# Value matmuls of two key steps in one run, one pair of adds by accumulating DMA, and a later normalisation, in a transformer block on one core

## The chip, the core and the metric

The kernel runs on one core of a Trainium2 chip. The core has a matrix engine (TensorE, PE in the profile, its weight loads as PEld), a vector engine (VectorE, DVE), an activation engine (ScalarE, ACT), a general engine (GpSimd, POOL) and a queue engine that only issues transfers here (SyncE, SP). Each takes its instructions in the order of its own queue and waits on semaphores for the others. The metric is the device time in microseconds; the median of three runs before is 1076.01 us (1075.66 to 1076.06).

## The reference

All data are float32. There are 2 sequences of 1024 tokens of width 512, 16 heads of 32, and a mixture of 8 experts with a shared one.

```python
q, k, v = (split(x @ W.T + b + 0.5 * (x @ Bm.T) @ Am.T) for W, b, Bm, Am in qkv)
attn = softmax(q @ k.T * HEAD_DIM ** -0.5)
x = layernorm(x + lora_linear(merge(attn @ v), Wo, bo, Bo, Ao))
# then: top-1 of 8 experts with capacity 256, gated, plus a shared expert
x = layernorm(x + moe(x))
```

## The kernel before

The program has three stages: the projections to q, k and v (about the first 160 us), attention (to about 628 us), and the experts. The change touches attention alone.

**Units and steps.** Attention runs over 16 units `u`: a group of four heads, `g = u // 2`, and one half of the queries (512 of them). A unit has 8 steps `kc`, one for each block of 128 keys; the loop at the end of the attention stage counts `t = 8 u + kc` up to 127. The order of the work is written out by hand: within this loop all five engines keep the order in which the program issues (`tc.manual_schedule(engines=MAN2)`), so every engine's queue is what the Python code says.

**What a step does.** `st_step` makes four score tiles, one per head: a matmul writes `st` (128 keys x 512 queries) into one of three PSUM banks of the pool `one`, and ScalarE writes its exponential into half of an exponential tile `pt` (128 x 2 x 512, two heads). Such tiles come from a pool of `PTB` buffers; `pts[t, pr]` is the tile of head pair `pr` at step `t`. Between the four heads other work is queued, in the lists `between[0]` to `between[3]`:

- `s1_step` works 12 steps ahead (`LEAD`). It makes score tiles `s` of a later unit the other way round (queries on the partitions) into three PSUM banks of the pool `s1p`, and VectorE takes each row's maximum (`mt`). The maxima of a unit end in `mx`, are turned by a transpose (`mp`) and go by two small DMAs into two extra rows of the query tile `qs`, so that the later matmul `st` subtracts them. There are four such tiles per step, up to step 115.
- `av_step(t - 1)` multiplies the exponentials of the step before with the values. A head's output is only 32 wide, so four heads fill the four column groups of TensorE and share one bank `av`; eight matmul instructions of the trace are one such run. There are two banks `av`.
- `add_step` sums the exponentials of steps 1 to 6 into the tiles of step 0 (`accs`), for the denominators. For most units ten adds go to GpSimd and two to VectorE (`ON_DVE`): (step 1, pair 0), queued early, at its own step, and (step 2, pair 1). The last two units have a division of their own (`DVE_END`).
- `finish(u - 1)`, at step `FIN` of the next unit, makes the column sums with a matrix of ones: sixteen matmul instructions over the tiles of step 7 and of the sums, directly behind a value run. ScalarE copies the result to `rc`, SP sends four rows to DRAM and back as `r16`.
- `invert(u - 1)`, after step `REC`, takes the reciprocal on VectorE; SP writes it out and broadcasts it to 32 partitions per head with four DMAs, as `rb`.
- `normalize(u - 1)` at step 7 multiplies the bank `av` by it on VectorE (`mult`, part 0), ScalarE makes the rounded half `at_h` (part 1), VectorE the rest `at_l` (`lo`, part 2).
- `add_res` adds a bias to the residual rows on GpSimd, mostly once per unit at its step 1; the rows were loaded three steps earlier. `oproj` is the output projection: of the first sequence from step 65 to step 81, of the second from step 126 on.

SP also loads the keys of a later head group, the queries of a later unit and the values at the beginning of units. Line numbers of the profile: 182 the tile `s`, 190 its maximum, 569 `st`, 578 the exponential, 588 the add, 599 the value matmul, 622 the sums, 636 to 653 the copy and the reciprocal with its transfers, 661 to 665 the normalisation, 674 the bias of the residual.

Of the kernel before, what the change touches and what calls it, by code (L numbers as in the profile page):

```python
# [9 lines left out]
F32 = mybir.dt.float32  # L10
# [3 lines left out]
ALU = mybir.AluOpType  # L14
# [4 lines left out]
P = 128  # L19
B, L, D = 2, 1024, 512  # L20
NU = 16
# [13 lines left out]
NS = NU * 8  # L35
WARM, WCOL = 4, 256
OPER = 4
PTB = 13
OHB = 3
LOADS = {  # L40
# [10 lines left out]
MAN4 = MAN2 - MAN3  # L51
DIRECT = (7,)
NO_DIR = (NU - 2,)
FIN = 3
REC = 4
XTB = 5
ON_DVE = ((1, 0), (2, 1))
EARLY = (1, 0)
OPROJ_AT = (65, 67, 69, 71, 73, 75, 77, 79)
RES_AT = tuple(8 * i + 6 for i in range(8)) + (70, 78, 86, 94, 98, 102, 106, 110)  # L60
RES_ADD = 3
# [7 lines left out]
FINE, NRME = 2, 4  # L69
DVE_END = {  # L70
    NU - 2: ((1, 0), (2, 1), (4, 1), (5, 1), (6, 0), (6, 1), (7, 0), (7, 1)),
    NU - 1: ((1, 0), (2, 0), (3, 0), (4, 0), (5, 0), (6, 0), (6, 1)),
}
# [19 lines left out]
def kernel(  # L93
# [3 lines left out]
    pe, act, dve, pool, sp = nc.tensor, nc.scalar, nc.vector, nc.gpsimd, nc.sync  # L97

    def f(ap):
        return ap.bitcast(F32)  # L100
# [41 lines left out]
    def load_k(g):  # L142
        kt = Ks[g % 2]
        for blk, hl in ((0, 0), (1, 1), (2, 0)):
            sp.dma_start(
                out=f(kt[32 * blk : 32 * blk + 32]),
                in_=qk_d[1, g // NG, g % NG, hl].rearrange("(h p) t -> p h t", p=32),
            )
# [13 lines left out]
    def load_q(u):  # L162
        g, qb = u // 2, u % 2
        for blk, hl in ((0, 0), (1, 0), (2, 1)):
            sp.dma_start(
                out=f(Qs[u % 3][32 * blk : 32 * blk + 32]),
                in_=qk_d[0, g // NG, g % NG, hl].rearrange("(h p) t -> p h t", p=32)[
                    :, :, qb * 512 : qb * 512 + 512
                ],
            )  # L170

    mts, pts, avs, accs, vts = {}, {}, {}, {}, {}
# [377 lines left out]
    with ph2, tc.manual_schedule(engines={mybir.EngineType.PE}):  # L550
        ptp = att_left.enter_context(
            tc.tile_pool(name="ptp", bufs=PTB, side="left", reuse_waits="tile")
        )
        ap = ph2.enter_context(
            tc.tile_pool(name="ap", bufs=1, side="right", reuse_waits="tile")
        )
# [25 lines left out]
        def add_step(t, pr):  # L582
            u, kc = t // 8, t % 8
            if kc == 0:
                accs[u, pr] = pts[t, pr]
            elif kc not in direct(u):
                eng = dve if (kc, pr) in DVE_END.get(u, ON_DVE) else pool
                eng.tensor_tensor(accs[u, pr], accs[u, pr], pts[t, pr], ALU.add)  # L588

        def early(t, pr):  # L590
            return t // 8 not in DVE_END and (t % 8, pr) == EARLY

        def av_step(t):
            u, kc = t // 8, t % 8
            g = u // 2
            if kc == 0:
                avs[u] = avp.tile([P, 512], F32, name=f"av{u}", tag="av")
            for h in range(4):
                pe.matmul(  # L599
                    avs[u][32 * h : 32 * h + 32, :],  # L600
                    vts[g][:, kc, 32 * h : 32 * h + 32],
                    pts[t, h // 2][:, h % 2, :],
                    start=kc == 0,
                    stop=kc == 7,
                    skip_group_check=True,
                )
            for pr in range(2):
                if not early(t, pr):
                    add_step(t, pr)

        def direct(u):
            return () if u in NO_DIR else DIRECT
# [3 lines left out]
        def finish(u):  # L616
            sm = one.tile([P, 512], F32, name=f"sm{u}", tag="one")
            parts = [lambda h, k_=k_: pts[u * 8 + k_, h // 2][:, h % 2, :] for k_ in direct(u)]
            parts.append(lambda h: accs[u, h // 2][:, h % 2, :])
            for i, pf in enumerate(parts):  # L620
                for h in range(4):
                    pe.matmul(
                        sm[32 * h : 32 * h + 32, :],
                        ones32,
                        pf(h),
                        start=i == 0,
                        stop=i == len(parts) - 1,
                        skip_group_check=True,
                    )
            if u >= RDIR:  # L630
                rc = ap.tile([P, 512], F32, name=f"rc{u}", tag="rc", bufs=1)
                dve.reciprocal(rc, sm)
                fin[u] = rc
                return
            rc = ap.tile([P, 512], F32, name=f"rc{u}", tag="rc", bufs=1)
            act.copy(rc, sm)
            sd = dram.tile([4, 512], F32, name=f"sd{u}")
            sp.dma_start(out=sd, in_=rc[0:P:32, :])
            r16 = ap.tile([P, 16], F32, name=f"r16_{u}", tag="r16", bufs=1)
            sp.dma_start(out=r16, in_=sd.rearrange("h (j c) -> (h j) c", c=16))  # L640
            fin[u] = r16

        def invert(u):
            r16 = fin[u]
            rd = dram.tile([4, 512], F32, name=f"rd{u}")
            dve.reciprocal(r16, r16)
            sp.dma_start(out=rd.rearrange("h (j c) -> (h j) c", c=16), in_=r16)
            rc = ap.tile([P, 512], F32, name=f"rb{u}", tag="rb", bufs=1)
            for h in range(4):
                sp.dma_start(  # L650
                    out=rc[32 * h : 32 * h + 32, :],
                    in_=rd[h : h + 1, :].partition_broadcast(32),
                )
            fin[u] = rc

        def normalize(u, parts=(0, 1, 2)):
            g, qb = u // 2, u % 2
            cs = slice(qb * 512, qb * 512 + 512)
            hi, lo = at_h[:, g % NG, cs], at_l[:, g % NG, cs]
            if 0 in parts:  # L660
                dve.tensor_tensor(avs[u], avs[u], fin[u], ALU.mult)
            if 1 in parts:
                act.copy(hi, avs[u])
            if 2 in parts:
                dve.tensor_tensor(lo, avs[u], f(hi), ALU.subtract)
# [38 lines left out]
        def run(gen):  # L704
            for _ in gen:
                pass
# [4 lines left out]
        for t in range(NS):  # L711
            u, k = t // 8, t % 8
            if k == 0:
                if u % 2 == 0 and 2 <= u and u // 2 + 1 < B * NG:
                    load_k(u // 2 + 1)
                if u >= 1 and u + 2 < NU:
                    load_q(u + 2)
                if u % 2 and NG <= u // 2 + 1 < B * NG:
                    load_v(u // 2 + 1)
            if t in RES_AT:  # L720
                load_res(RES_AT.index(t))
            between = [[], [], [], []]
            if early(t, 0):
                between[2].append(lambda: add_step(t, 0))
            if t + LEAD < NS:
                for q in range(4):
                    between[q].append(lambda q=q: s1_step(t + LEAD, q))
            elif t + LEAD == NS:
                between[0].append(lambda: finish_max(NU - 1))
            if t:  # L730
                between[1].append(lambda: av_step(t - 1))
                if u and k == (FINE if u == NU - 1 else FIN):
                    between[1].append(lambda: finish(u - 1))
            if u:
                if k == (NRME if u == NU - 1 else 7):
                    between[0].append(lambda: normalize(u - 1, (0,)))
                    between[1].append(lambda: normalize(u - 1, (1,)))
                    between[2].append(lambda: normalize(u - 1, (2,)))
            if t - RES_ADD in RES_AT:
                between[3].append(lambda: add_res(RES_AT.index(t - RES_ADD)))  # L740
            st_step(t, between)
            if k == REC and 1 <= u < NU - 1:
                invert(u - 1)
            if t in OPROJ_AT:
                op0 = oproj(0, OPROJ_AT.index(t), OPER)
            if OPROJ_AT[0] <= t:
                next(op0, None)
            if t + 1 in OPROJ_AT[1:]:
                run(op0)
            for _, fn in [x for x in later if x[0] == 0]:  # L750
                fn()
            later[:] = [(n - 1, fn) for n, fn in later if n]
            if t - NS >= OPROJ1:
                next(op10, None)
        av_step(NS - 1)
        finish(NU - 1)
        normalize(NU - 1, (0,))
        run(op10)
# [301 lines left out]
    for st in range(NB):  # L1060
# [18 lines left out]
        if st == NB - 3:  # L1079
            reads_xd(  # L1080
                sp.dma_start(
                    out=meta, in_=xd_d[:, D : D + 2].rearrange("(j p) c -> p j c", p=P)
# [7 lines left out]
    with tc.manual_schedule(engines=MAN4):  # L1090
        last = None
        for e in range(E):
            nxt = e + 1
            hss = []
            for c in range(6):
# [32 lines left out]
                if e:  # L1128
                    for hf in range(2):
                        j = 2 * (e - 1) + hf  # L1130
# [7 lines left out]
        for hf in range(2):  # L1138
            j = 2 * (E - 1) + hf
# [65 lines left out]
```

## Time and profile before

| what | value |
|---|---|
| median of three runs | 1076.01 us |
| the profiled execution's own time | 1076.59 us |
| its span, first to last instruction | 1074.9 us |
| mean granted TensorE clock | 0.993 |
| a unit of attention (units 1 to 7, 11, 12) | 27.8 us |
| units 8 and 9, with output projections | 37.6 and 40.0 us |
| maximum of one tile `s` on VectorE | 512 x, mean 0.680 us |
| add on GpSimd | 151 x, mean 2.413 us |
| add on VectorE | 43 x, mean 2.131 us |

One execution is profiled; durations and waits come from it. A busy TensorE in the profile is not one at its peak, since matmuls are pipelined and their ends modelled; distances between starts tell more. In a row the form is: engine, line, operation, out<-in by the program's names (buffer numbers left out), shapes and count. In a timeline the first two columns are the start and the length in us, and a bracket at the end names the idle time before and who ended it. In the table by window the columns are the window, its length, then the busy time of PE, PEld, DVE, ACT and POOL with the number of instructions, the granted clock, the busy share of the DMA engines and their GB/s.

### The profile page before, as it was taken

Reading aid. Unit: us, or ns where it says so; the run is one execution under the profiler, and the core shown is the slowest. Engines: PE = TensorE matmul, PEld = TensorE weight load, DVE = VectorE, ACT = ScalarE, POOL = GpSimd, SP = SyncE. Lnnn points to the kernel's source line nnn. Section 1 sums busy time; section 2 is a strip of 40 time slices with the busy share of each in tenths; the row PEclk is TensorE's granted clock in tenths of the full one; section 3 lists DMA queues with packets and bytes.
Section 4 is the critical chain, followed back from the end, with each engine's and each line's share of the span. In section 5 each row is a group of like instructions: output and inputs, shape, how many; then the busy total and the mean of one; then the engine's idle time right before and its main releaser. Section 6 shows DMA issues by size and latency. Waiting matters only on the chain. (4 is left out here: it accounts for less than half of the span.)

```text
span 1074.9 us, 16446 instructions
## 1 busy us (share of the span) xinstructions
PE 1038.9 (97%) x5992; PEld 742.9 (69%) x5992; DVE 748.3 (70%) x1217; ACT 530.1 (49%) x1026; POOL 573.1 (53%) x379
## 2 busy tenths in 40 slices
PE   8999999999999999999999999999999999999996
PEld 6888774444444455544444369889999998888885
DVE  6732788999999987799998784233522556777762
ACT  5422215666666655556666756222222455555552
POOL 5000007888888877868899575000050045666674
PEclk8999999999999999999999999999999999999999
DMA  8866860141414242042520123000082556777731
GB/s 279 288 219 202 252 195 25 52 110 48 103 47 106 71 109 70 22 90 70 119 81 22 51 60 109 20 21 20 31 240 95 161 184 207 234 234 235 237 107 59
DMA packets 77585, 131.24 MB, mean 122 GB/s; under 512 B 14344, under 2 KB 23048, under 8 KB 77504
## 3 DMA queue, kind: packets, MB, share of 16 engines
q1 hardware_dynamic: 73664, 117.59, 37.6%
q0 software_dynamic: 3840, 12.60, 3.3%
q8 instruction: 47, 0.77, 0.3%
q14 instruction: 34, 0.28, 0.1%
HBM read 96.10 MB, written 33.80 MB: 121 GB/s over the span
## 5 line engine op out<-in xcount | busy, mean ns | idle before, releaser
L588 POOL TENSOR_TENSOR pt<-pt,pt 128x1024 f32<-128x1024 f32 x151 | 360.5, 2413 | 207.7 <-ACT pt L578 190.6
L190 DVE TENSOR_REDUCE mt<-s 128x1 f32<-128x512 f32 x512 | 323.4, 680 | 39.7 <-PE s L182 39.6
L578 ACT ACTIVATE pt<-st 128x512 f32<-128x512 f32 x512 | 270.8, 602 | 141.4 <-PE st L569 137.6
L569 PE MATMUL st<-qs,ks 98*128 98x512 f32 x512 | 215.6, 432 | 1.9 <-ACT pt L578 1.2
L182 PE MATMUL s<-ks,qs 96*128 96x512 f32 x512 | 203.0, 404 | 12.7 <-DVE mt L190 11.5
L569 PEld LDWEIGHTS st<-qs,ks 98*128 98x128 f32 x512 | 96.0, 189 | 136.4 <-issue 87.2
L817 POOL TENSOR_TENSOR w2s<-w2r,w2s 128x512 fp32r<-128x512 f32 x42 | 65.7, 1582 | 127.0 <-ACT w2s L816 103.1
L829 PE MATMUL h<-xthe,w13s 128*128 128x256 f32 x704 | 131.4, 284 | 1.5 <-DVE hs L850 1.5
L182 PEld LDWEIGHTS s<-ks,qs 96*128 96x128 f32 x512 | 97.2, 190 | 41.3 <-DVE mt L190 26.8
L829 PEld LDWEIGHTS h<-xthe,w13s 128*128 128x128 f32 x704 | 111.0, 191 | 3.0 <-DVE hs L850 2.7
L829 PE MATMUL h<-xtle,w13s 128*128 128x256 f32 x352 | 100.2, 285 | 0.0
L588 DVE TENSOR_TENSOR pt<-pt,pt 128x1024 f32<-128x1024 f32 x43 | 91.4, 2131 | 3.3 <-ACT pt L578 2.9
L599 PE MATMUL av<-pt,vt 128*32 128x512 f32 x512 | 75.0, 605 | 0.0
L599 PE MATMUL av<-pt,x1b 128*32 128x512 f32 x512 | 68.8, 609 | 0.0
L829 PEld LDWEIGHTS h<-xtle,w13s 128*128 128x128 f32 x352 | 67.3, 191 | 0.7
L977 POOL DMA_INDIRECT xd_d<-x1a,slot_i x8 | 8.0, 996 | 111.8 <-DVE slot_i L974 109.7
L873 PE MATMUL y<-w2s,hs 128*128 128x512 f32 x260 | 62.7, 394 | 2.9 <-POOL w2s L817 2.9
L873 PEld LDWEIGHTS y<-w2s,hs 128*128 128x128 f32 x260 | 47.4, 188 | 15.7 <-POOL w2s L817 6.7
L297 PE MATMUL o<-xh,wh 128*128 128x512 f32 x128 | 51.1, 399 | 3.0 <-ACT wh L271 3.0
L312 ACT ACTIVATE oh<-o,bqk_sb 128x512 fp32r<-128x512 f32 x32 | 22.0, 690 | 59.0 <-PE o L297 56.5
L297 PE MATMUL o<-xl,wh 128*128 128x512 f32 x128 | 50.9, 398 | 0.0
L297 PE MATMUL o<-xh,wl 128*128 128x512 f32 x128 | 50.9, 397 | 0.0
(819 smaller groups left out, 1758.5 us busy)
## 6 DMA issues: line engine op xcount, KB each, us to landing
qs<-qkd SPq DMA_DIRECT2D x48, 256.0 KB, 5.6
ks<-qkd SPq DMA_DIRECT2D x24, 512.0 KB, 6.8
x1a<-in_w_dram SPq DMA_DIRECT2D x24, 512.0 KB, 6.8
w2r<-in_w_dram SPq DMA_DIRECT2D x42, 256.0 KB, 3.2
qkd<-oh SPq DMA_DIRECT2D x32, 256.0 KB, 2.7
qkd<-ol SPq DMA_DIRECT2D x32, 256.0 KB, 2.6
x1b<-in_w_dram SPq DMA_DIRECT2D x16, 512.0 KB, 5.7
x1b<-in_wT_dram SPq DMA_DIRECT2D x16, 256.0 KB, 5.3
```

The source lines that it names most:

```text
L182: pe.matmul(s1, Qs[u % 3][0:96, h, qt * P : qt * P + P], Ks[g % 2][0:96, h, kh * 512 : kh * 512 + 512], start=True, stop=True,)
L190: dve.tensor_reduce(mts[u][:, c, kh : kh + 1], s1, AX.X, ALU.max)
L297: pe.matmul(o, lhs, rhs, start=k + i == 0, stop=k + i == KC + 1)
L312: act.activation(oh, o, AF.Identity, bias=bias)
L569: pe.matmul(sb, Ks[g % 2][:, h, kc * P : kc * P + P], Qs[u % 3][:, h, :], start=True, stop=True,)
L578: act.activation(pts[t, h // 2][:, h % 2, :], sb, AF.Exp, scale=SCALE)
L588: eng.tensor_tensor(accs[u, pr], accs[u, pr], pts[t, pr], ALU.add)
L599: pe.matmul(avs[u][32 * h : 32 * h + 32, :], vts[g][:, kc, 32 * h : 32 * h + 32], pts[t, h // 2][:, h % 2, :], start=kc == 0, stop=kc == 7 ...
L817: pool.tensor_tensor(hl[:, 1, :], raw, f(hl[:, 0, :]), ALU.subtract)
L829: pe.matmul(hp[:, j * 256 : j * 256 + 256], lhs, rhs[:, k, :], start=n == 0, stop=n == 11,)
L873: pe.matmul(o, lhs, rhs, start=n == 0, stop=n == 16)
L977: sc_ = pool.indirect_dma_start(out=xd_d, out_offset=bass.IndirectOffsetOnAxis(ap=slot_i[:, i : i + 1], axis=0), in_=x1[i // 8][:, i % 8, ...
```

## The change

`av_step` of two key steps is now issued together, at every even step: at step t those of t - 2 and t - 1, and after the loop those of the last two steps. The adds leave `av_step` and get a function `adds`, called at every step with a table `ADDS` by key step. In units 0 to 13 the tiles of step 4 are added to those of step 5 by two DMAs from GpSimd's queue that accumulate into their destination; step 6 is added before step 5, and the tiles of step 5, which hold both, one step later. One add in twelve stays on VectorE, (step 1, pair 0), without its early place. The last two units keep their division.

The sums move from step 3 to step 4 of the next unit (in the last unit they stay at step 2), the reciprocal from behind step 4 to behind step 5, the normalisation from step 7 of the next unit to step 0 of the one after it; in the last unit it stays at step 4 for unit 14, and unit 13's comes at its step 0. The broadcast reciprocal takes the buffer of `rc` instead of one of its own, and the exponential tiles are 14 instead of 13.

```diff
-PTB = 13
+PTB = 14
...
-FIN = 3
-REC = 4
+FIN = 4
+REC = 5
+NRM = 0
 XTB = 5
-ON_DVE = ((1, 0), (2, 1))
-EARLY = (1, 0)
+ON_DVE = ((1, 0),)
+ADDS = {
+    0: ((0, 0, 0), (0, 0, 1)), 1: ((0, 1, 0), (0, 1, 1)), 2: ((0, 2, 0), (0, 2, 1)),
+    3: ((0, 3, 0), (0, 3, 1)), 5: ((0, 4, 0), (0, 4, 1)), 6: ((0, 6, 0), (0, 6, 1)),
+    7: ((0, 5, 0), (0, 5, 1)),
+}
...
-            for pr in range(2):
-                if not early(t, pr):
+
+
+        def adds(t):
+            u, kc = t // 8, t % 8
+            if u in DVE_END:
+                for pr in range(2):
                     add_step(t, pr)
+                return
+            for v, j, pr in ADDS.get(kc, ()):
+                i = (u - v) * 8 + j
+                if i < 0 or u - v in DVE_END:
+                    continue
+                if j == 4:
+                    pool.dma_start(out=pts[i + 1, pr], in_=pts[i, pr], accum_op=ALU.add)
+                else:
+                    add_step(i, pr)
...
-            rc = ap.tile([P, 512], F32, name=f"rb{u}", tag="rb", bufs=1)
+            rc = ap.tile([P, 512], F32, name=f"rb{u}", tag="rc", bufs=1)
...
-            if early(t, 0):
-                between[2].append(lambda: add_step(t, 0))
...
             if t:
-                between[1].append(lambda: av_step(t - 1))
+                if t % 2 == 0:
+                    between[1].append(lambda: (av_step(t - 2), av_step(t - 1)))
+                between[1].append(lambda: adds(t - 1))
                 if u and k == (FINE if u == NU - 1 else FIN):
                     between[1].append(lambda: finish(u - 1))
             if u:
-                if k == (NRME if u == NU - 1 else 7):
-                    between[0].append(lambda: normalize(u - 1, (0,)))
-                    between[1].append(lambda: normalize(u - 1, (1,)))
-                    between[2].append(lambda: normalize(u - 1, (2,)))
+                for v in [u - 2] * (k == NRM and u > 1) + [u - 1] * (u == NU - 1 and k == NRME):
+                    between[0].append(lambda v=v: normalize(v, (0,)))
+                    between[1].append(lambda v=v: normalize(v, (1,)))
+                    between[2].append(lambda v=v: normalize(v, (2,)))
...
+        av_step(NS - 2)
         av_step(NS - 1)
+        adds(NS - 1)
         finish(NU - 1)
```

More of the change, by code (lines that the diff above doesn't have):

```diff
@@ L588, in add_step @@
                 eng.tensor_tensor(accs[u, pr], accs[u, pr], pts[t, pr], ALU.add)
-        def early(t, pr):
-            return t // 8 not in DVE_END and (t % 8, pr) == EARLY
         def av_step(t):
```

## The prediction

> **What bounds the kernel now.** I read the page first, its busy line and slices:
>
> ```profile
> PE 1038.9 (97%) x5992; PEld 742.9 (69%) x5992; DVE 748.3 (70%) x1217; ACT 530.1 (49%) x1026; POOL 573.1 (53%) x379
> ...
> PE   8999999999999999999999999999999999999996
> PEld 6888774444444455544444369889999998888885
> DVE  6732788999999987799998784233522556777762
> ...
> POOL 5000007888888877868899575000050045666674
> ```
>
> In slices 6 to 22 (about 160 to 600 us, the attention steps) PE, DVE and POOL are all near full; the change lives there. So I asked for the engines' busy time by unit (window, length, then PE, PEld, DVE, ACT, POOL busy):
>
> ```profile
> 355.00:382.80 27.80, 27.16 (x146) 13.08 (x145) 25.77 (x40) 17.79 (x36) 24.78 (x12) 1.00 0.26 68
> 382.80:420.40 37.60, 36.46 (x187) 20.53 (x185) 31.56 (x53) 19.46 (x38) 30.96 (x20) 1.00 0.36 80
> 420.40:460.40 40.00, 38.70 (x194) 22.09 (x194) 32.70 (x57) 21.45 (x40) 28.41 (x20) 1.00 0.19 49
> ```
>
> Units 1 to 7 and 10 to 13 are like the first line, 27.8 us; units 8 and 9 also carry output projections. Nobody has more than 3 us free. The PE timeline shows where a step goes:
>
> ```profile
> 355.70 0.39 PE L182 MATMUL s<-ks,qs 96*128 96x512 f32 x1
> 356.02 1.06 PE L599 MATMUL av<-pt,x1b 128*32 128x512 f32 x8
> 357.01 0.50 PE L569 MATMUL st<-qs,ks 98*128 98x512 f32 x1
> 357.35 0.40 PE L182 MATMUL s<-ks,qs 96*128 96x512 f32 x1
> 357.58 0.40 PE L569 MATMUL st<-qs,ks 98*128 98x512 f32 x1
> ...
> 361.58 0.40 PE L569 MATMUL st<-qs,ks 98*128 98x512 f32 x1
> 362.13 0.49 PE L182 MATMUL s<-ks,qs 96*128 96x512 f32 x1
> ```
>
> Full-width matmuls start 0.235 us apart. Around a value run the distances are 0.32, 0.99 and 0.34. Where sums follow the value run directly, their first matmul comes 0.88 after it began, so a run of eight is 0.88 of work and about 0.31 of entering and leaving (0.085 + 0.11 + 0.105). At 362.13 PE waits for a reduction. VectorE shows why:
>
> ```profile
> 360.24 1.23 DVE L588 TENSOR_TENSOR pt<-pt,pt 128x1024 f32<-128x1024 f32 x1
> 361.38 2.48 DVE L190 TENSOR_REDUCE mt<-s 128x1 f32<-128x512 f32 x4
> 364.32 2.48 DVE L190 TENSOR_REDUCE mt<-s 128x1 f32<-128x512 f32 x4 [0.46 <-PE s L182]
> 366.72 3.36 DVE L588 TENSOR_TENSOR pt<-pt,pt 128x1024 f32<-128x1024 f32 x1
> ```
>
> and GpSimd's timeline beside it:
>
> ```profile
> 361.83 7.16 POOL L588 TENSOR_TENSOR pt<-pt,pt 128x1024 f32<-128x1024 f32 x3 [1.71 <-ACT pt L578]
> ```
>
> The same add costs VectorE 1.23 us with GpSimd idle, and 3.36 inside GpSimd's train of adds: it ends 1.08 after the train does. A step without a wait is 3.06 us, so a unit is 8 x 3.06 + 1.72 (sixteen sum matmuls) + 1.6 of stalls.
>
> **What the Trainium skill says.** "TensorEngine Tiling (Array Packing)", Key Properties: changing the tiling mode drains TensorE; the 0.31 above agrees. "SBUF — State Buffer", Who interferes with whom: a VectorE instruction with two SBUF inputs and a GpSimd one that reads SBUF exclude each other for a whole instruction; 3.36 against 1.23 agrees. "DMA: Bandwidth & Descriptors", Anatomy of one DMA: a GpSimd DMA takes about 2.0 us + bytes/436e3; "Collectives: The Full Stack", The bandwidth ceiling: an add in the DMA needs two source reads. No accumulating DMA runs before, so neither is shown here for one.
>
> **The change, part by part.**
>
> Value runs. Eight per unit become four: 4 x 0.31 = 1.25 us less PE work. Two steps take 14 x 0.235 + 0.32 + 1.86 + 0.34 = 5.80 instead of 6.12. But the eight reductions now meet score tiles s in one bunch. With tile 0 at time 0, tiles come 0.47 apart; a reduction starts 0.43 after its tile, lasts 0.68, the next begins 0.60 later; there are three s buffers, and a tile started 0.06 after the reduction three earlier ended (tile 362.13, reduction 362.07). Reductions 0 to 4 end at 1.11, 1.71, 2.31, 2.91, 3.51, so tiles 5, 6, 7 may start at 2.37, 2.97, 3.57 instead of 3.29: 0.28 late per bunch. VectorE catches up only during the run, idle part of it. Before, bunches of four never filled the buffers. So 1.1 of the 1.25 is given back.
>
> Normalisation, moved from step 7 to step 0 two units on: same instructions. Its subtraction `lo` falls behind the first reduction of a bunch, shifts the rest by 0.60, and tile 7 comes 0.60 later still. Its input chain on SP (reciprocal to multiply: 374.3 to 381.3 before) keeps its two steps; sums and reciprocal moved together. A late broadcast would hold VectorE and with it s. The projections from step 65 find unit 6 normalised at step 64 instead of 63, a step of 4 us ahead.
>
> Sums a step later: same sixteen matmuls, now behind an even step's run; nothing gained. SP's queue order is unchanged, the max rows still behind the sums' small DMAs, four steps ahead of use.
>
> VectorE adds. The 3.36 us one goes; most of the 1.6 us of stalls was its doing. The (1,0) add loses its early place: it is queued before the step's third reduction, and waits for the value run of tile 0, since it overwrites that tile. Counted from tile 7: VectorE is through with its reductions, `lo` included, at 1.65; the run's first half is done at about 1.4. Free, the add ends at 2.8, before the next reduction can begin (2.52 + 0.43): cost 0. If GpSimd has just begun its own (1,1) add, released by the same run, VectorE is through at 3.85 + 1.1 = 4.95: 2.0 us late, all of it PE time.
>
> GpSimd. Ten adds of 2.38 become nine, plus two DMA issues. Indirect DMA issues in this trace take 0.96 us, 1.27 apart; I bound one issue by 0.5 and 2 and take 1.2: no net gain. The issues wait for the value run of step 5 (the DMA writes tiles 5), and all adds queue behind them. From there: 2.4 + four adds 9.4 + a residual add 1.3 = 13.1 us, against about 12.2 to the value run at step 2. So GpSimd is still in its residual add when VectorE wants the port, and the wait is some tenths. I take 0.8 between the ends 0 and 2.0.
>
> Landing. An estimate from the two pages: 512 KiB at twice the reads, 2.0 + 2.4 = 4.4, two together up to 7; 512 KB loads here land in 5.5 to 6.8. The adds of tiles 6 run ahead of those of tiles 5 and cover 4.7 + the second issue. I take 6: hidden. The fourteenth exponential tile allows the longer life of tiles 4 and 5; in the built order step 2's exponentials wait for the landing and step 3's for the adds of tiles 5.
>
> Unit: 4 x 5.80 + 1.72 + 0.2 (transpose) + 1.1 + 0.6 + 0.8 = 27.6, 0.2 less than now; eleven units: -2.2. Unit 0: -0.5. Units 8 and 9: projections spread the tiles, so the 1.25 stays, and of 2.0 and 2.5 us of stalls (step times over 4 x 8.95 + 1.72, the first step of unit 8 having none) I take 1 each: -4.5.
>
> Last eleven steps, no s left. ACT waits once per step for the scores behind a value run:
>
> ```profile
> 603.88 2.07 ACT L578 ACTIVATE pt<-st 128x512 f32<-128x512 f32 x4 [0.65 <-PE st L569]
> 606.59 0.60 ACT L578 ACTIVATE pt<-st 128x512 f32<-128x512 f32 x1 [0.64 <-PE st L569]
> ```
>
> Once per two steps saves 5 x 0.65 = 3.2. The adds there exclude each other (unit 15: 7 x 1.08 + 5 x 2.38 = 19.5 us of port in about 21.3), so I take half: -1.5. The second run behind the last step, 0.9 us, falls into the wait of the last sums for their adds.
>
> Sum: -2.2 - 0.5 - 4.5 - 1.5 = -8.7. The profiled execution took 1076.59 (span 1074.9), the median 1076.01: 1067.9 for a profiled one, **1067** for the median. Behind attention PE is full (slices 25 to 39), so the shift passes through.
>
> **The rivals.**
>
> Full gain: the port is always free and the end keeps its 3.2. Unit 26.8: 11 x -1.0 - 0.5 - 5.5 - 3.2 = -20, 1056. For it: where both waited for the port (587.14, 620.41) VectorE got it first. Against: `lo` makes it late.
>
> No change: the bunches eat the drains and the port wait is 1.1, the projection units only just gain: 1074 to 1078.
>
> GpSimd idle at the value run of step 2 (issue at 0.5): 2.0 each unit, 28.8: 11 x 1.0 - 4.5 - 1.5 = +5, 1081.
>
> Slower by landing: GpSimd's loop is issue 1.2 + landing L + 2 adds 4.7 + residual 1.3 + (1,1) behind the lock 3.4 + 4 adds 9.5 = 20 + L, which passes 27.8 at L about 8 us. At L = 10 about 29.5 to 30: 11 x 1.9 - 4.5 = +16, 1092. For it: two reads per element beside 0.75 to 2.3 MB of loads at each unit's start. Against: the estimate of 7 and the gap of more than a step before those loads.
>
> **How the numbers follow.** Forecast 0.42 (own range 1061 to 1073), full gain 0.18, no change 0.11, idle GpSimd 0.12, landing 0.17. A measurement here tells 0.2%, 2.15 us, from no change. Faster 0.60, same 0.11, slower 0.29. Leaving out half of the full gain and half of the late landings gives 1056 to 1088.
>
> **What would show it.** Right: 64 value runs of 16; odd steps near 1.9 and even ones near 4.2 in place of 3.06; a step with `lo` near 2.5; VectorE adds of 1.2 to 2.4, one per unit; landings under 7 us; units of about 27.6. Wrong: VectorE adds of 3.3, ACT waiting for a landing or for adds of tiles 5, VectorE waiting for the broadcast rb, or bunches without a late tile 7.

## The result, and the profile after

The changed kernel took 1110.62 us, median of four runs (1107.94 to 1111.42), against 1076.03 for the kernel before beside it: 1.0317 times as long, 95% interval 1.0299 to 1.0336. The forecast was 1067, with a range of 1056 to 1088. The profiled execution took 1110.09 us, its span 1108.4.

The busy line and four slices of the page of the changed kernel:

```profile
PE 1047.0 (94%) x5992; PEld 743.5 (67%) x5992; DVE 711.7 (64%) x1203; ACT 531.5 (48%) x1026; POOL 579.4 (52%) x393
...
PE   8999999989898999999899799999999999999995
...
DVE  6732888868686786678877686332432556777752
...
POOL 4000009879787887587879586100050035666674
PEclk8999999999898999999999899999999999999998
```

The clock's line of the page before was level through attention:

```profile
PEclk8999999999999999999999999999999999999999
```

As many matmuls as before take 8 us longer although half of the drains around the value runs are gone, and PE's slices and its granted clock (PEclk) now have dents between slices 6 and 24. The same window view as before, for units 2 to 5 (window, length, then PE, PEld, DVE, ACT, POOL busy, clock, share of the DMA engines, GB/s):

```profile
210.20:242.40 32.20, 28.80 (x146) 13.33 (x145) 23.76 (x39) 18.16 (x37) 24.83 (x13) 0.95 0.57 123
242.40:269.70 27.30, 27.03 (x146) 12.89 (x146) 22.50 (x39) 17.78 (x36) 25.11 (x13) 1.00 0.43 90
269.70:303.20 33.50, 29.68 (x147) 13.46 (x146) 23.93 (x39) 18.21 (x37) 24.89 (x13) 0.90 0.55 119
303.20:331.30 28.10, 27.25 (x146) 12.89 (x145) 23.42 (x39) 18.13 (x37) 25.09 (x13) 1.00 0.39 84
```

These odd units are about as forecast (27.6), the even ones are 5 to 6 us longer, with PE waiting and with less than the full clock. PE's timeline of unit 4's step 4 (start, length, and in brackets the idle time before with who ended it):

```profile
283.81 0.40 PE L574 MATMUL st<-qs,ks 98*128 98x512 f32 x1
287.12 0.76 PE L187 MATMUL s<-ks,qs 96*128 96x512 f32 x1 [2.91 <-DMA qs<-qkd]
287.68 0.63 PE L574 MATMUL st<-qs,ks 98*128 98x512 f32 x1
288.11 0.63 PE L187 MATMUL s<-ks,qs 96*128 96x512 f32 x1
288.67 3.42 PE L601 MATMUL av<-pt,x1b 128*32 128x512 f32 x16
```

PE waits 2.9 us for a query tile, and what follows runs at half speed: this paired value run takes 3.42 us, an undisturbed one in unit 3 (at 250.54 us) 1.92. Line 187 at this place is the first `s` tile of unit 6, which reads the keys and queries that SP began to load at the start of unit 4. The transfers issued from 266 to 277 us, by queue and by kind, in the changed kernel (q0 is GpSimd's queue, q1 that of SP; in a row of a queue stand packets, MB and the share of the DMA engines' time):

```profile
q0 software_dynamic: 284, 1.05, 57.0%
q1 hardware_dynamic: 614, 1.08, 27.1%
issues: line engine op xcount, KB each, median us to landing
ks<-qkd SPq DMA_DIRECT2D x3, 512.0 KB, 11.0
pt<-pt POOLq DMA_DIRECT2D x2, 512.0 KB, 7.8
qs<-qkd SPq DMA_DIRECT2D x3, 256.0 KB, 12.4
```

SP's timeline in the same window:

```profile
269.58 2.55 SPq L150 DMA_DIRECT2D ks<-qkd  x3
272.18 3.72 SPq L170 DMA_DIRECT2D qs<-qkd  x3
```

For comparison, the loads of unit 4 in the kernel before, issued from 266 to 277 us there:

```profile
ks<-qkd SPq DMA_DIRECT2D x3, 512.0 KB, 6.7
qs<-qkd SPq DMA_DIRECT2D x3, 256.0 KB, 10.9
```

and SP's timeline of that kernel at the start of its unit 6:

```profile
327.14 1.26 SPq L145 DMA_DIRECT2D ks<-qkd  x3
328.45 1.71 SPq L165 DMA_DIRECT2D qs<-qkd  x3
```

In these 11 us the accumulating DMAs move about as many bytes as SP's queue and take twice its share of the DMA engines. The issues of the six loads stretch from 3.0 to 6.3 us. The last query transfer of units 2, 6 and 12 lands 16.7 to 18.1 us after the unit's start, where the kernel before had 12.7 to 13.7, and the first `s` tile of step 4 is due there at 14.1 to 14.6. Unit 8 is a control: its tile lands at 16.9 us, its steps are longer, step 4 starts at 17.5, and PE doesn't wait. The Trainium skill, "DMA: Bandwidth & Descriptors", Queues, rings and completion order, says that a DMA engine takes the queues that have work in turn, packet by packet; the slowed loads fit that, though no run here shows the turn itself.

By groups of units (sums of the unit times, in us; the last two columns are experiments told below):

| stretch | before | after | without the DMAs | shorter key loads |
|---|---|---|---|---|
| unit 0 | 29.8 | 24.6 | 24.6 | 24.6 |
| units 2, 4, 6, 12 | 111.4 | 133.2 | 110.4 | 114.9 |
| units 1, 3, 5, 7, 11, 13 | 167.4 | 168.8 | 168.1 | 174.3 |
| units 8 to 10 | 107.6 | 112.9 | 112.6 | 112.8 |
| unit 14 to the first expert matmul | 77.9 | 85.3 | 82.2 | 84.4 |
| sum | 494.1 | 524.8 | 497.9 | 511.0 |

Of the 33.5 us between the two profiled spans, 31.1 lie ahead of the first expert matmul (652.2 us before, 683.3 after); the expert stage, which the change doesn't touch, is 2.4 longer in this profile.

### The profile page after: what moved, and what is told of

Its sections match the earlier page's. It is cut to its first block, busy times and chain, and to the rows that moved or that the text cites. A ratio compares the mean times of both kernels' runs of the same rounds, so it can differ in the third digit from the quotient of the medians.

```text
span 1108.4 us, 16460 instructions
## 1 busy us (share of the span) xinstructions
PE 1047.0 (94%) x5992; PEld 743.5 (67%) x5992; DVE 711.7 (64%) x1203; ACT 531.5 (48%) x1026; POOL 579.4 (52%) x393
## 5 line engine op out<-in xcount | busy, mean ns | idle before, releaser
L593 POOL TENSOR_TENSOR pt<-pt,pt 128x1024 f32<-128x1024 f32 x137 | 339.7, 2626 | 189.2 <-DVE mt L195 148.9
L195 DVE TENSOR_REDUCE mt<-s 128x1 f32<-128x512 f32 x512 | 319.6, 679 | 92.2 <-PE s L187 91.9
L187 PE MATMUL s<-ks,qs 96*128 96x512 f32 x512 | 220.2, 437 | 29.0 <-DVE mt L195 16.1
L574 PE MATMUL st<-qs,ks 98*128 98x512 f32 x512 | 211.2, 422 | 4.5 <-ACT pt L583 3.6
L601 PE MATMUL av<-pt,vt 128*32 128x512 f32 x512 | 67.1, 640 | 0.3 <-DVE at_l L680 0.3
L601 PE MATMUL av<-pt,x1b 128*32 128x512 f32 x512 | 65.6, 632 | 0.0
L593 DVE TENSOR_TENSOR pt<-pt,pt 128x1024 f32<-128x1024 f32 x29 | 54.6, 1894 | 11.8 <-ACT pt L583 8.4
L622 POOL DMA_DIRECT2D pt<-pt x28 | 25.1, 1041 | 48.4 <-PE st L574 45.4
```

The source lines that it names most:

```text
L187: pe.matmul(s1, Qs[u % 3][0:96, h, qt * P : qt * P + P], Ks[g % 2][0:96, h, kh * 512 : kh * 512 + 512], start=True, stop=True,)
L195: dve.tensor_reduce(mts[u][:, c, kh : kh + 1], s1, AX.X, ALU.max)
L574: pe.matmul(sb, Ks[g % 2][:, h, kc * P : kc * P + P], Qs[u % 3][:, h, :], start=True, stop=True,)
L601: pe.matmul(avs[u][32 * h : 32 * h + 32, :], vts[g][:, kc, 32 * h : 32 * h + 32], pts[t, h // 2][:, h % 2, :], start=kc == 0, stop=kc == 7 ...
L622: pool.dma_start(out=pts[i + 1, pr], in_=pts[i, pr], accum_op=ALU.add)
```

## The experiments

Theory A: the accumulating DMAs make the key and query loads late, TensorE waits for them at step 4 of the even units and then runs at half clock (units 8 and 10 aside, which have more time). Rival B: the paired runs themselves cost. Rival C: the later normalisation and late GpSimd and VectorE work hold TensorE up. In some of the runs the expert stage took 433 to 438 us instead of 423 to 425, and the kernel before beside them was longer too (1088 us against 1076 to 1077); why is not known. So besides the ratio to the kernel before beside them I compare the start of the first expert matmul and the units. Forecasts in us suppose 1076 for the kernel before.

**The DMAs away** (tile 4 is left out of the sums, and 1 is added to them so that none is zero).

```diff
-                    pool.dma_start(out=pts[i + 1, pr], in_=pts[i, pr], accum_op=ALU.add)
+                    continue
...
-            act.copy(rc, sm)
+            act.activation(rc, sm, AF.Identity, bias=ones32[:, 0:1], scale=1.0)
```

> The changed kernel without its 28 accumulating DMAs: tile 4 is left out of the denominators of units 0 to 13 (and 1 is added to these sums, so that none is zero), so the output is not the reference's; everything else, the paired value runs and the late normalisation included, stays. Theory A (the DMAs delay the key and query loads that the first s tile of unit u+2 needs at step 4 of the even units, and TensorE waits there some 3 us and then runs at a lower granted clock): units 2, 4, 6 and 12 fall from 32.2 to 33.8 us to about 27.6, so about 23 us come back and the wait on the query tile goes: 1080 to 1090 us. Rival B (the paired value runs are what costs): nothing but a few us comes back, 1103 us or more. Rival C (the sums and the normalisation a step later hold VectorE and the rest up): also 1103 or more.

Measured: 1.0061 (1.0043 to 1.0079), first expert matmul at 655.8 us. Units 2 and 3 in the window view:

```profile
213.70:241.10 27.40, 27.01 (x146) 12.99 (x145) 22.59 (x39) 18.04 (x37) 23.34 (x11) 1.00 0.46 104
241.10:268.50 27.40, 27.02 (x147) 13.00 (x145) 22.43 (x39) 18.00 (x37) 23.52 (x11) 1.00 0.20 55
```

Even and odd units alike take 27.4 us, 0.4 less than before the change, but for unit 4 (28.3) and unit 1. The DMAs, with their issues and waits, cost 27 of the 31 us, and B falls as the main cause. What stays is in units 8 to 10, in the end, and in unit 1 (31.3 us), where VectorE's one add of the unit met GpSimd's. VectorE's timeline of this run, then GpSimd's:

```profile
191.21 3.46 DVE L593 TENSOR_TENSOR pt<-pt,pt 128x1024 f32<-128x1024 f32 x1
```

```profile
191.20 2.38 POOL L593 TENSOR_TENSOR pt<-pt,pt 128x1024 f32<-128x1024 f32 x1 [1.48 <-ACT pt L583]
```

VectorE began some 0.01 us later, so it stood through GpSimd's whole add and took 2.38 + 1.08 us. PE then waited 1.61 us for a row maximum, and the clock was halved for 6.8 us.

**One value run a step again, with the DMAs.**

```diff
-                if t % 2 == 0:
-                    between[1].append(lambda: (av_step(t - 2), av_step(t - 1)))
+                between[1].append(lambda: av_step(t - 1))
```

> The changed kernel with one value run in every step again (the value matmuls of the step before, as in the kernel before), its accumulating DMAs, sums, normalisation and 14 tiles kept; nothing is left out. Theory A: the waits on the query tile at step 4 of units 2, 4, 6 and 12 stay, 3 to 4.5 us each with the lower clock behind them; only the gain of the pairing is lost and units 8 and 9 come back: 1100 to 1115 us. Rival B: the time falls to about 1076 to 1082. Rival C: 1100 or more, but with waits on the normalised tiles instead of the query tile.

Measured: 1.050 (1.044 to 1.056), slower than the changed kernel, so B is out as the main cause from this side too. My forecast of A missed: in units 2, 4 and 6 the query tile costs hardly anything here. The waits of VectorE in units 2 to 6, and those of PE over attention:

```profile
DVE av L676 <- DMA rb<-rd: 10.8, 5, 3.5
```

```profile
PE s L187 <- DVE mt L195: 28.8, 23, 3.3
...
PE s L187 <- DMA qs<-qkd: 0.5, 1, 0.5
```

VectorE stands in its queue for the broadcast reciprocal `rb`, its row maxima come late, and PE waits for them, ahead of step 4, which starts 16.4 to 20.1 us into these units. By then the loads are there. This is C, and it does not contradict A: in unit 12, where step 4 starts at 14.1 us, PE waits 3.25 us at the same first `s` tile (the profile names no releaser for this wait).

**The same DMAs in the kernel before** (units 0 to 6, onto the spare `wo_l`, since two scratch tiles of their own had no room: the pool would have taken 44.4 kb per partition where 38.7 were left):

```diff
                 if not early(t, pr):
                     add_step(t, pr)
+                if kc == 5 and pr == 0 and u < 7:
+                    for c in range(2):
+                        pool.dma_start(
+                            out=f(wo_l[:, 2 * c : 2 * c + 2, :]),
+                            in_=f(wo_h[:, 2 * c : 2 * c + 2, :]),
+                            accum_op=ALU.add,
+                        )
```

> The kernel before, and in each of units 0 to 6 two accumulating DMAs of 512 KB on GpSimd's queue, issued in step 6 as in the changed kernel; they add wo_h onto the spare low half of the output weights (wo_l), which nothing reads before unit 8, so the output comes out wrong from the projection on; nothing else is changed or left out. Theory A (these DMAs delay the key and query loads of the even units; TensorE waits at their step 4 and then runs at half clock): units 2, 4 and 6 rise from 27.8 us to 30 to 34 us, PE waits for the query tile there by 1 to 4 us, and the whole rises by 8 to 20 us, with no value run paired. If the DMAs cost only their issues on GpSimd: every unit within 0.5 us of before, the whole within 3 us.

Measured: 1.035 (1.029 to 1.042); first expert matmul at 679.6, 27 us later than before. So the DMAs alone cost as much in a kernel that pairs nothing, but the way was not the one I forecast: units 3 to 7, odd ones too, take 31.7 to 33.8 us, and no unit waits over 0.3 us for the query tile. The loads are slowed here too, as A says: SP's six issues take 5.3 to 5.6 us in units 2, 4 and 6, and 3.0 in unit 12, ahead of which there is no such DMA. But step 4 starts 15.7 to 20.6 us into those three units (14.4 before), which gives the loads time. GpSimd's timeline of unit 4, and VectorE's:

```profile
274.77 1.73 POOL L612 DMA_DIRECT2D wo_l<-wo_h  x2
275.92 7.69 POOL L588 TENSOR_TENSOR pt<-pt,pt 128x1024 f32<-128x1024 f32 x3
...
284.20 2.74 POOL L588 TENSOR_TENSOR pt<-pt,pt 128x1024 f32<-128x1024 f32 x1
```

```profile
282.61 5.42 DVE L588 TENSOR_TENSOR pt<-pt,pt 128x1024 f32<-128x1024 f32 x1
287.96 2.47 DVE L190 TENSOR_REDUCE mt<-s 128x1 f32<-128x512 f32 x4
```

Two issues more, and adds behind them of about 2.6 instead of 2.4 us each, make GpSimd's train late, VectorE's add stands 5.42 us until the train leaves it the port, and PE waits 4.34 us for a maximum.

**The DMAs two steps earlier** (tiles 2 onto tiles 3 in step 4; tiles 4, 5, 6 and 3 by engines):

```diff
-    3: ((0, 3, 0), (0, 3, 1)), 5: ((0, 4, 0), (0, 4, 1)), 6: ((0, 6, 0), (0, 6, 1)),
-    7: ((0, 5, 0), (0, 5, 1)),
+    3: ((0, 2, 0), (0, 2, 1)), 4: ((0, 4, 0), (0, 4, 1)), 5: ((0, 5, 0), (0, 5, 1)),
+    6: ((0, 3, 0), (0, 3, 1)), 7: ((0, 6, 0), (0, 6, 1)),
...
-                if j == 4:
+                if j == 2:
```

(Tile 2's entry for step 2 is dropped.)

> The changed kernel with its two DMAs a unit moved two steps ahead: tiles 2 are added to tiles 3 by DMAs in step 4, and tiles 4, 5, 6 and then 3 by engines; as many DMAs, adds and bytes, nothing left out. Theory A: the DMAs, issued some 13 us after the unit's start, land by 24 us, ahead of the next unit's loads; the query tile is in time at step 4 of units 2, 4, 6 and 12, which come at 27.3 to 28.5 us; first expert matmul at 655 to 664 us instead of 683, ratio 1.005 to 1.013. If it is the DMAs' traffic or issue as such and not where it falls: as slow as the changed kernel, ratio 1.025 to 1.035.

Measured: 1.063 (1.060 to 1.066), worse than either expectation. The query wait is gone, as A says, and SP's six issues take 2.8 to 3.7 us again (step 4 also starts later, at 16.5 to 17.1). But VectorE now waits for the small transfer of the sums, beside which the DMAs fall. VectorE's waits from 213 to 420 us (units 2 to 7):

```profile
DVE r L661 <- DMA r<-sd: 14.8, 7, 3.4
```

So each of the two places tried makes a neighbour late, not the same one.

**Tile 4 by GpSimd, no DMAs** (and the second half of tile 2 by VectorE, as before the change):

```diff
-ON_DVE = ((1, 0),)
+ON_DVE = ((1, 0), (2, 1))
...
-                if j == 4:
-                    pool.dma_start(out=pts[i + 1, pr], in_=pts[i, pr], accum_op=ALU.add)
-                else:
-                    add_step(i, pr)
+                add_step(i, pr)
```

> The changed kernel with tile 4 added by GpSimd again, both halves, in the place of the two DMAs, and the second half of tile 2 by VectorE as in the kernel before (10 adds of GpSimd and 2 of VectorE a unit, no DMA); pairing, late sums and normalisation stay and nothing is left out. Theory A: no wait on the query tile, even units as short as odd ones, about 27.6 us, units 8 and 9 as in the changed kernel (4 us longer together than before): 1076 to 1088 us. Rival B: 1100 or more. Rival C, in the form that GpSimd's lateness is what holds TensorE: more waits for exponential tiles, 1095 or more.

Measured: 1.058 (1.056 to 1.059); C's number was right, A's wrong. As A says, no wait for the query tile is left; but PE waits for row maxima, and not for exponential tiles as C had it. VectorE's timeline in unit 3, then PE's:

```profile
265.56 3.09 DVE L593 TENSOR_TENSOR pt<-pt,pt 128x1024 f32<-128x1024 f32 x1
```

```profile
269.30 0.66 PE L187 MATMUL s<-ks,qs 96*128 96x512 f32 x1 [2.88 <-DVE mt L195]
269.89 3.39 PE L601 MATMUL av<-pt,x1b 128*32 128x512 f32 x16
```

VectorE's (2, 1) waits for GpSimd's (1, 1), which changes the same tile, and starts just behind GpSimd's next add. In most units PE then waits 2.7 to 2.9 us, and the clock is halved again. So this run brought a loss of its own, and A's number could not be tested with it.

**One run a step in the projection's steps alone.**

```diff
-                if t % 2 == 0:
+                if 65 <= t <= 80:
+                    between[1].append(lambda: av_step(t - 1))
+                elif t % 2 == 0:
```

> The changed kernel with one value run a step in steps 65 to 80 alone, where the projection's matmuls lie in the odd steps; all else as changed, nothing left out. If the row add and statistics of the projection stand ahead of VectorE's bunched reductions in an odd step that has no value run to cover them: units 8 and 9, now 39.5 and 41.7 us, come back to 37.5 to 38.5 and 40, so 3 to 4 us in all and a ratio of about 1.028. If the rise of these units is from the DMAs or the later normalisation: no change, 1.032.

Measured: 1.032 (1.027 to 1.038), too wide to tell 4 us. The units do:

```profile
393.20:430.70 37.50, 37.24 (x195) 20.91 (x194) 29.57 (x53) 19.78 (x38) 30.77 (x19) 1.00 0.60 130
430.70:468.90 38.20, 37.94 (x194) 22.02 (x193) 29.62 (x55) 21.48 (x39) 27.43 (x22) 1.00 0.35 77
```

75.7 us for units 8 and 9, where the changed kernel has 81.2 and the kernel before 77.6, with the DMAs still in. In unit 9 the odd steps take 4.0 us in both, with a value run or without one, and the even ones (but for the one with the sums) 5.8 with two and 4.9 with one: pairing saved nothing in the odd steps there. VectorE's timeline of an odd step of the changed kernel's unit 9 shows what the odd step's value run used to cover:

```profile
450.75 0.69 DVE L711 TENSOR_TENSOR x1a<-op,x1a 128x512 f32<-128x512 f32 x1 [1.06 <-PE op L706]
451.47 0.69 DVE L536 BATCH_NORM_STATS2 sta<-x1a 128x6 f32<-128x512 f32 x1
...
452.56 2.47 DVE L195 TENSOR_REDUCE mt<-s 128x1 f32<-128x512 f32 x4
```

**The `s` tiles two steps later.**

```diff
-LEAD = 12
+LEAD = 10
```

> The changed kernel with the first-pass score tiles two steps later (12 steps ahead becomes 10), so that the query tile loaded at an even unit's start is first read in its step 6, some 6 to 8 us later; the DMAs, their place and everything else stay, nothing is left out. Theory A (late loads make TensorE wait at step 4 of units 2, 4, 6 and 12): no wait on the query tile, these units at 27.3 to 28.5 us in the place of 32.2 to 33.8, first expert matmul at 658 to 666 us in the place of 683, ratio 1.008 to 1.018. If the accumulating DMAs cost by another way (GpSimd's lateness, VectorE's waits for small transfers): even units stay above 30 us, ratio 1.025 or more.

Measured: 1.106 (1.103 to 1.109). No wait on the loaded query tile is left, but the row maxima now reach their rows too late; PE's waits:

```profile
PE st L574 <- DMA qs<-ml: 77.7, 14, 7.0
```

The experiment brought a larger wait of its own and tells nothing of A.

**One DMA a unit** (the other half of tile 4 is left out; 1 is added to the sums as in the first run).

```diff
+                if j == 4 and pr == 1:
+                    continue
```

> The changed kernel with one accumulating DMA a unit instead of two: the second half of tile 4 is left out of the denominators (1 is added to these sums so that none is zero), so the output is not the reference's; all else stays. Theory A with bytes as the cause: the loads are late by half as much, 1 to 2 us of wait where it was 3 to 4.5, units 2, 4, 6 and 12 at 28.5 to 31 us, first expert matmul at 661 to 673 us, ratio 1.012 to 1.022. If a threshold decides (1 to 2 us of slack are enough for one DMA): all of these units at 27.4 to 28 us and the ratio of the kernel without DMAs, 1.006. If the number of bytes doesn't matter: 1.028 or more.

Measured: 1.026 (1.024 to 1.028), first expert matmul at 678.6. In units 4, 6 and 12 PE still waits 2.2 to 2.9 us at the first `s` tile of step 4 (2.9 to 4.1 after the change); units 1, 2 and 11 come at 31 us by VectorE's add beside GpSimd's, as unit 1 in the run without DMAs. The wait was not halved, but the lateness nearly was: the last query transfer of units 2, 6 and 12 lands 15.3 to 16.1 us after the unit's start, 2.4 to 2.8 later than in the kernel before, where two DMAs made it 3.9 to 5.4. The tile is due earlier here, at 13.4 us in units 4, 6 and 12 in the place of 14.1 to 14.6, and that takes back the rest. Bytes and the number of DMAs were halved together, so which of them sets the lateness is not shown.

**Shorter loads, DMAs kept.** Two of the three key loads are left out from unit 2 on (the rows of the low-order terms among them).

```diff
-                    load_k(u // 2 + 1)
+                    load_k(u // 2 + 1, 1)
```

> The changed kernel with one of the three 512 KB key loads at the start of each even unit from unit 2 on; the other two are left out, so these rows of the key tile stay those of an earlier head group and the output is not the reference's. All engine work, the accumulating DMAs and their place stay. Theory A (the loads' bytes share the DMA engines with the accumulating DMAs and come too late for step 4): 1 MB less to land, no wait on the query tile, units 2, 4, 6 and 12 at 27.3 to 28.5 us, first expert matmul at 656 to 664 us, ratio 1.006 to 1.014. If the accumulating DMAs cost by GpSimd's or VectorE's waits instead: these units stay above 31 us, ratio 1.025 or more.

Measured: 1.0169 (1.0151 to 1.0187), first expert matmul at 668.1. The windows of units 4, 6 and 7:

```profile
267.50:295.60 28.10, 27.43 (x146) 12.90 (x145) 23.32 (x39) 18.19 (x37) 24.92 (x13) 1.00 0.47 105
323.70:353.90 30.20, 28.31 (x146) 14.12 (x145) 24.61 (x39) 18.21 (x37) 24.90 (x13) 0.94 0.42 92
353.90:386.80 32.90, 29.32 (x147) 14.47 (x145) 22.71 (x39) 17.96 (x37) 24.96 (x13) 0.90 0.43 95
```

No query wait; units 2, 4, 6 and 12 get 18 of their 22 us back, so late loads are what held them. But the odd units, 3 and 7 above all, lose 5.5 us more than in the changed kernel; VectorE stands there for `rb`, up to 4.8 us, where it was 2.5 at most in the changed kernel (from 213 to 420 us: total, times, longest):

```profile
DVE av L676 <- DMA rb<-rd: 9.4, 3, 4.8
```

It is issued 2.3 and 1.5 us ahead of units 3 and 7, where the changed kernel has 2.7 and 2.3; that explains only part of the lateness, and the rest is open. So A is one of at least two ways in which the DMAs cost, and the second grew when the first was taken away.

**Looking for a version that gains.** First without DMAs and without VectorE's add: tiles 6 and 7 go into the sums directly, in step 2; one value run a step in steps 65 to 80.

```diff
-DIRECT = (7,)
+DIRECT = (6, 7)
...
-FIN = 4
-REC = 5
+FIN = 2
+REC = 4
...
-ON_DVE = ((1, 0),)
+ON_DVE = ()
...
-    3: ((0, 3, 0), (0, 3, 1)), 5: ((0, 4, 0), (0, 4, 1)), 6: ((0, 6, 0), (0, 6, 1)),
-    7: ((0, 5, 0), (0, 5, 1)),
+    3: ((0, 3, 0), (0, 3, 1)), 5: ((0, 4, 0), (0, 4, 1)), 6: ((0, 5, 0), (0, 5, 1)),
...
-                if j == 4:
-                    pool.dma_start(out=pts[i + 1, pr], in_=pts[i, pr], accum_op=ALU.add)
-                else:
-                    add_step(i, pr)
+                add_step(i, pr)
```

> A version without the DMAs and without an add on VectorE: tiles 6 and 7 go into the sums' matmuls as they are, tiles 1 to 5 are added by GpSimd, the sums are made in step 2 of the next unit, value runs are paired but for steps 65 to 80; nothing is left out. Four more sums' matmuls a unit, about 0.43 us. If the loads and the two-engine adds are all that held the pairing up: units at 27.4 + 0.4 = 27.8 us and no wait over 1 us, units 8 and 9 as before, the whole within 0.4% of the kernel before. If pairing costs by itself: a ratio over 1.01.

Measured: 1.0012 (1.0004 to 1.0021). PE has no wait over 1 us until unit 14; most units take 28.2 us, 0.4 more than forecast, which eats the gain of unit 0. Unit 14 loses 3.5, in a wait of 4.0 for the last row maximum. So one run a step from step 113 on:

```diff
-                if 65 <= t <= 80:
+                if 65 <= t <= 80 or t > 112:
```

> The version without DMAs and without VectorE's add (tiles 6 and 7 in the sums as they are, sums in step 2), with one value run a step from step 113 on as well; nothing left out. If the 4.0 us wait of TensorE for the last row maximum in unit 14, and the half clock after it, come from the paired run there: unit 14 at 26.9 to 27.5 us in the place of 30.4, first expert matmul at 648 to 649.5 in the place of 652.8, ratio 0.995 to 0.998. If it has another cause: 1.000 to 1.002 as before.

Measured: 1.0008 (0.9999 to 1.0017); the wait stayed, 3.4 us, behind a VectorE add of 3.11 that began 0.34 us after GpSimd's. Next, both halves of tile 1 of that unit by VectorE:

```diff
-    NU - 2: ((1, 0), (2, 1), (4, 1), (5, 1), (6, 0), (6, 1), (7, 0), (7, 1)),
+    NU - 2: ((1, 0), (1, 1), (4, 1), (5, 1), (6, 0), (6, 1), (7, 0), (7, 1)),
```

> The version without DMAs, with one value run a step in steps 65 to 80 and from 113 on, and in unit 14 both halves of tile 1 added by VectorE in the place of the second half of tile 2, whose add waits for GpSimd's and ran 3.1 us beside GpSimd's; nothing left out. If that add is what makes TensorE wait 3.4 us for the last row maximum: unit 14 at 26.9 to 27.6 us in the place of 30.9, first expert matmul at 649.5 to 651 us, ratio 0.996 to 0.998. If not: 1.000 to 1.002.

Measured: 1.0012 (0.9998 to 1.0027). Its windows of units 14 and 15:

```profile
570.10:597.50 27.40, 26.40 (x146) 11.34 (x145) 21.66 (x28) 17.49 (x35) 22.63 (x10) 1.00 0.17 50
597.50:623.00 25.50, 22.67 (x96) 8.49 (x95) 19.51 (x15) 16.06 (x32) 12.48 (x5) 0.87 0.00 1
```

Unit 14 is as forecast (30.9 us without this edit), so that add was what made PE wait there; and unit 15 pays: 25.5 us where the kernel before has 20.8, with PE waiting 2.8 us for `at_l`, behind two VectorE adds of 3.39 and 3.22. Last, the kernel before with unit 0 alone paired:

```diff
 DVE_END = {
+    0: ((1, 0),),
...
-                between[1].append(lambda: av_step(t - 1))
+                if t > 8:
+                    between[1].append(lambda: av_step(t - 1))
+                elif t % 2 == 0:
+                    between[1].append(lambda: (av_step(t - 2), av_step(t - 1)))
```

> The kernel before with the value runs of unit 0 alone paired (and the second add of VectorE and its early add left to GpSimd in that unit): the one place where the changed kernel gained 5 us; nothing is left out. If that gain is of the pairing (TensorE's 2.2 us wait in unit 0, with its half clock, is gone): unit 0 at 24.6 to 25.5 us in the place of 29.8, all other units as in the kernel before, ratio 0.995 to 0.996. If it is of something else in the change: unit 0 at 27 to 30 us, ratio 0.998 to 1.001.

Measured: 1.0041 (1.0027 to 1.0055). Unit 0 at 24.6 us, and then unit 1, VectorE's timeline:

```profile
189.24 8.74 DVE L589 TENSOR_TENSOR pt<-pt,pt 128x1024 f32<-128x1024 f32 x1
```

It stands until GpSimd has done the adds that the shorter unit had no time for; PE waits 7.8 us, and unit 1 takes 38.0. With two tiles' adds taken from GpSimd there:

```diff
-            return () if u in NO_DIR else DIRECT
+            return () if u in NO_DIR else DIRECT if u else (6, 7)
...
-                if u and k == (FINE if u == NU - 1 else FIN):
+                if u and k == (FINE if u == NU - 1 else FIN if u > 1 else 2):
```

> The kernel before with the value runs of unit 0 alone paired, and in unit 0 tiles 6 and 7 taken into the sums as they are, in step 2 of unit 1, so that GpSimd has 9 adds there and not 11 (4 more sums' matmuls, about 0.43 us, in unit 1); nothing left out. If the loss in unit 1 of the last such run was GpSimd's debt: unit 0 at 24.6 us, unit 1 at 27.8 to 28.6, all other units as in the kernel before, first expert matmul at 647 to 648 us, ratio 0.995 to 0.9965. If the gain in unit 0 is always paid later: 0.999 or more.

Measured: 0.9996 (0.9984 to 1.0008); unit 0 at 24.6 and unit 1 at 32.0, with one wait of 2.0. No version tried beats the kernel before.

## Why the prediction was wrong

- **TensorE's sum, right.** Odd steps without a wait take 1.9 to 2.0, even ones 4.2, the step with `lo` 2.6. Without DMAs a unit is 27.4 us where I had 27.6. Two readings of the page were loose, without much weight: ScalarE has 10 us of a unit free, and unit 10 took 30.0 before, not 27.8.
- **Landing, where it failed.** I asked what the loads at a unit's start do to the accumulating DMAs, in the landing rival, and wrote that SP's queue order is unchanged. I never asked what the DMAs do to these loads, and so put their lateness at nothing. In the kernel before the last query transfer landed at 12.7 to 13.7 us and its first reader came at 14.6: that was all the slack. With the DMAs the landing came 3.9 to 5.4 us later, PE waited 2.5 to 4.1 us at step 4 of units 2, 4, 6 and 12, and with the half clock behind it these four units took 21.8 us more than before. The sums' move, for which I wrote "nothing gained", also took slack from this reader: without the DMAs, and with the sums in step 4, it comes at 13.2 us. The DMAs' own landing was also worse than my 6 us (4.8 to 10.3, median 7.2), but GpSimd waited at most 2.1 us for it. The rival slower by landing had the right sign, less than half of the size (+16 against +34.6), and the wrong mechanism.
- **The late broadcast.** I named it as a way to be wrong and gave it no time. It holds VectorE for up to 2.5 us in the changed kernel, and for up to 4.8 with two key loads left out.
- **Projection units, wrong sign.** Forecast -4.5, measured +3.6 for units 8 and 9. I counted the drains there and not the cover: 1.8 us of row add and statistics stand ahead of four bunched reductions in an odd step that has lost its value run, and the step still takes 4.0 us.
- **Unit 0, too small.** Forecast -0.5, measured -5.2: PE's wait of 2.2 us there, with its half clock, disappears.
- **The end.** Forecast -1.5, measured +7.4. I counted ScalarE's small waits and not the last row maximum, for which PE waits 4.0 us. Why the versions of the changed kernel without DMAs still lose 4.3 to 6.7 us there is only partly settled: VectorE's adds beside GpSimd's are seen in each, and moving one moved the wait from unit 14 to unit 15.
- **VectorE's add, the range right, its price wrong.** I had 0 to 2.0 us of PE time. A PE wait of 1.61 us in the run without DMAs cost 3.9, since the clock fell. No term of the sum had the clock in it, though the window of unit 0 before the change would have shown 0.94.

## What to carry to other kernels

When a transfer is added, list every transfer that is under way from its issue to its landing, with the time at which each is due; here loads with 1 to 2 us of slack paid, and small round trips where the loads did not. Where an engine is as full as TensorE here (97%), price a wait of 1.5 us or more at about twice its length, as the clock mostly falls with it: the waits of units 2, 4, 6 and 12 after the change, and of unit 1 without DMAs, cost 1.6 to 2.4 times their length, against the 27.4 us of a unit without them. And before two short jobs are bunched, write down what work of other engines each of them covered.

## What the runs showed of the hardware

- **The clock falls after short waits.** Over the sixteen profiles of this case, in attention: of 117 PE waits of 0.5 to 1.2 us 14 had a clock of 0.5 during them or within 4 us, of 11 of 1.2 to 1.5 us 8, of 95 of 1.5 us or more 88. It stayed for 3.4, 6.8 or 10.2 us. The Trainium skill, "TensorE: Matmul & The Clock Gate", HAM oscillation — how this bites in real kernels, puts the rule at idle gaps over about 3.4 us; here 21 of the 23 waits of 1.5 to 2 us had the half clock with them, and so had 19 of the 21 that stand alone (no other wait of 0.5 us or more within 7 us). For this kernel the measured figure is the one to go by.
- **Accumulating DMAs of 512 KB from SBUF to SBUF** land after 4.8 to 10.3 us when two are issued together (5.2 to 6.2 when one is), take GpSimd 0.87 to 1.28 us to issue, and in the 11 us shown their packets took twice the DMA engines' time of plain transfers of about the same size (57.0% against 27.1% for 1.05 and 1.08 MB).
- **GpSimd's adds behind such an issue** are mostly recorded at about 3.0 us instead of 2.38 in the changed kernel.
- **Two-input adds of VectorE and GpSimd.** The Trainium skill, "SBUF — State Buffer", Who interferes with whom, says that a VectorE instruction with two SBUF inputs contends with a GpSimd one that reads SBUF, and that the order of issue decides who is blocked. In the run without DMAs a VectorE add that began about 0.01 us after GpSimd's took 3.46 us, one 0.04 us ahead of it 1.21, and GpSimd's then 3.4.
